# Graph attention in two layers: three row terms as column-tile partial sums, a later end of layer norm, and another order of the first transposes

## The chip, the cores and the metric

The kernel runs on one core of one Trainium2 chip. The metric is the device time of one execution in microseconds; smaller is better. A measured time is the median of several executions of the same program. The profile is of one execution.

## The reference

There are 4096 nodes with 512 features (`x`), an adjacency of zeros and ones (`adj`, 4096 x 4096), and two layers, each followed by adding its input and a layer norm over the 512 features without learned factors.

Layer 0 has 8 heads of 64 features:

```python
feats = jnp.einsum('nf,hfo->hno', X, W)
s_self = jnp.einsum('hno,ho->hn', feats, a_self)
s_neigh = jnp.einsum('hno,ho->hn', feats, a_neigh)
dense = s_self[:, :, None] + s_neigh[:, None, :]
dense = jnp.where(dense > 0, dense, ALPHA * dense)
dense = dense * A[None, :, :]
attn = jax.nn.softmax(dense, axis=-1)
out = jnp.einsum('hij,hjo->hio', attn, feats) + b[:, None, :]
```

Then `x = layernorm(x + relu(out))`. Layer 1 is an attention inside groups of 128 nodes: query, key and value are linear maps of x with biases, and

```python
a = jnp.where(mask, query @ key.T * scale, 0.0)
scores = (a + b + edge_encoding) * jnp.where(mask, 1.0, -1000000.0)
softmax = jax.nn.softmax(scores, axis=-1) * mask
return softmax @ value
```

with `b` and `edge_encoding` both the adjacency. Its result is added to x and normalized again.

## The kernel before, in words

The work lies in `adjacency_streamed_path`; a general path follows only for inputs of another kind and isn't run here. TensorE's instructions stand in the order in which the program was written (`manual_schedule` for that engine). The order on the other engines (VectorE, ScalarE, GpSimd, and SyncE, which issues most loads) is chosen when the program is built, from a model of times[...]. So a change in the text can move instructions on those engines that it doesn't name.

**Setup** (about 0 to 165 us) goes over eight blocks `k` of 512 rows of x. `load_rows` brings four tiles of 128 rows. `turn_rows` (L634) transposes them, chunk of features by chunk (outer loop `c`, inner loop over the four tiles `u`, L637 to L639), and ScalarE copies each chunk to `xT`, adding the row sums into `xs` (L640). `features` (L716, products L719) multiplies `xT` with W and VectorE adds the bias into `fb` (L727). `scores` (L644, products L648) multiplies with `wa`, which VectorE makes at the start from W and the two attention vectors (L628, L631); it puts four products of 32 columns each into four groups of 32 partitions, and ScalarE copies the result to `st` (L656). `exponentials` (L658) sums the four groups with a small product (L662) and takes exponentials. `scaled_features` (L730) makes `gst` and `fst` (ScalarE L741, then VectorE L742), which GpSimd's queue writes to memory (L754). After the last block, sixteen products of one column each (L789) multiply W with the sum `xsum` of all rows of x, four chunks of features for each of four pairs of heads; the result becomes `S_col` (L796). Then the first adjacency tiles are transposed (L1109) and cast by ScalarE to `at` (L1113).

**Four passes** over the adjacency follow (`main_pass`, L1287), one for each pair of heads, each over four chunks of 1024 columns and, inside, over 32 row tiles `j` in cycles of 8 tiles (passes 0 to 2) or 4 (pass 3, then called a group). In each cycle VectorE makes `q` (L1348) for each `j` and each of two heads; ScalarE (and, for one `j` in four and the second head, VectorE) makes a mark from it (L1357, L1353). TensorE computes `accf` from `at` (L1368), `acc` from `q` (L1388), and every eight tiles `dens` from the marks (L1402). There are six buffers for `q` in pass 3 and eight in the others. Between these products other pieces are put in: in pass 1 the weights of layer 1, in passes 1 to 3 the check of the adjacency (loads of `ck`, squares and absolute values on ScalarE, L1128 and L1129).

**Weights of layer 1** (`weights_of_layer_1`, L868) is a generator; `run_pieces` (L1273) takes its next piece while a credit lasts, and the numbers that it yields are what a piece costs of that credit. Its end has three row terms. `zb` is Wk times bq, made with sixteen one-column products (L912). `cb` is bk times bq (L928). `ub` is a row, Wq times bk: four products of 32 columns each put partial sums into four groups of 32 partitions (L932), ScalarE scales and copies them (L936), and one product with a matrix `pick`, which has ones in the rows 0, 32, 64 and 96, adds them into every partition (L943). These three stand in one piece on TensorE, at 951 to 961 us.

**Layer 1** is worked off block by block of 512 rows (`layer_1`, L948) from the second chunk of pass 3 on: as soon as a chunk of 1024 columns is done, its rows are assembled (`rows_of_layer_0`, L1133) in two blocks. There, VectorE takes the statistics and GpSimd the power (L524 to L528); what remains is a function `finish` (L530), which normalizes the four tiles `x1b` in place on VectorE (L532). It is kept as `plan["F"]` (L1145) and called at a place of its own. `layer_1` then transposes `x1b` (L954), ScalarE copies to `x1T` (L955), and products with M (L974), scores (L1001), values (L1046, bias added on VectorE L1054 as `v_t`) and the output (L1060) follow.

Where these pieces go in pass 3 is written out by hand. `PLAN` (L1256) has, for each of the eight groups of a chunk, two strings: what is put in ahead of `acc` and what behind it. `E` ends a chunk, and assembles the first block; `R` assembles the second; `F` calls the kept end of layer norm; `a` and `b` take the next part of the first and second block's layer 1. After the last chunk the same letters stand in one string (L1456).

Of the kernel before, what the change touches and what calls it, by code (L numbers as in the profile page):

```python
# [10 lines left out]
F32 = mybir.dt.float32  # L11
# [3 lines left out]
OP = mybir.AluOpType  # L15
# [4 lines left out]
P = 128  # L20
# [384 lines left out]
def adjacency_streamed_path(  # L405
# [80 lines left out]
    nc.gpsimd.memset(neg_half_4, -0.5)  # L486
    neg_quarter = const.tile([P, 1], F32, name="neg_quarter")
    nc.gpsimd.memset(neg_quarter, -0.25)
    ones_col = const.tile([P, 1], F32, name="ones_col")
    nc.gpsimd.memset(ones_col, 1.0)  # L490
    ident_b = const.tile([P, P], BF16, name="ident_b")
# [60 lines left out]
    def misc(shape, dtype=F32):  # L552

        banks.append(banks.pop(0))
        return banks[-1].tile(shape, dtype, name="ps_m")
# [4 lines left out]
    def ring(name, pool, n):  # L560
# [4 lines left out]
        turns[name] += 1  # L565
        return pool if k < n else more[name][0]

    ats = {}
    a_bs = {}
    pools = {}  # L570
# [11 lines left out]
    with tc.tile_pool(name="setup1", bufs=1, side="right") as one, tc.tile_pool(  # L582
# [50 lines left out]

        def turn_rows(k):  # L634
            xT = xTs[k] = two.tile([P, FC, 4, P], F32, name="xT_f")
            for c in range(FC):
                pt = pss.tile([P, 4, P], F32, name="ps_set")  # L637
                for u in range(4):
                    nc.tensor.transpose(pt[:, u, :], xts[k][u][:, ts(c, P)], ident)  # L639
                nc.scalar.activation(  # L640
                    xT[:, c], pt, AF.Identity, accum_out=xs[:, c, k : k + 1]
                )
# [114 lines left out]
        for k in range(NB):  # L757
            if k + 1 < NB:
                load_rows(k + 1)
            fbs = [features(k, 0)]  # L760
            if k == 0:
                fbs.append(features(k, 1))
                scores(0)
            else:
                exponentials(k)
            if k + 1 < NB:
                turn_rows(k + 1)
            if k == 0:
                exponentials(0)
            scaled_features(k, 0, fbs[0])  # L770
            if k:
                fbs.append(features(k, 1))
                columns_of_exponentials(k - 1)
            scaled_features(k, 1, fbs[1])
            fbs.append(features(k, 2))
            scaled_features(k, 2, fbs[2])
            if k + 1 < NB:
                scores(k + 1)
            rows_of_exponentials(k)
            fbs.append(features(k, 3))  # L780
            scaled_features(k, 3, fbs[3])
            if k in (3, 4, 5):
                tc.keep_in_program_order(load_adjacency(0, 4 * (k - 3)))
        xsum = one.tile([P, FC], F32, name="xsum")
        nc.vector.tensor_reduce(xsum, xs, AX.X, OP.add)
        pS = pss.tile([P, PR], F32, name="ps_set")
        for r in range(PR):
            for c in range(FC):
                nc.tensor.matmul(  # L789
                    pS[:, r : r + 1],  # L790
                    w_sb[:, c, ts(r, FP)],
                    xsum[:, c : c + 1],
                    start=(c == 0),
                    stop=(c == FC - 1),
                )
        nc.vector.scalar_tensor_tensor(  # L796
            S_col, b_col, float(N), pS, op0=OP.mult, op1=OP.add
        )
# [69 lines left out]
    def weights_of_layer_1(keep, wp):  # L868
# [33 lines left out]
        for o in range(FC):  # L902
# [3 lines left out]
            nc.scalar.copy(L1["wvT"][:, :, ts(o, P)], pv)  # L906
            if o % 2:
                yield 1.3
        pz = misc([P, FC])
        for m in range(FC):  # L910
            for o in range(FC):
                nc.tensor.matmul(  # L912
                    pz[:, m : m + 1],
                    ws["k"][:, o, ts(m, P)],
                    cols["q"][:, o : o + 1],
                    start=(o == 0),
                    stop=(o == FC - 1),
                )
        nc.scalar.mul(L1["zb"], pz, scale)
        yield 2.0  # L920

        pc = misc([P, 1])
        kb = wp.tile([P, FC, P], F32, name="kb")
        nc.vector.tensor_copy(kb, cols["k"][:, :, None].to_broadcast([P, FC, P]))

        pu = misc([P, F])
        for o in range(FC):
            nc.tensor.matmul(  # L928
                pc, kb[:, o, :], cols["q"][:, o : o + 1], start=(o == 0), stop=(o == FC - 1)
            )  # L930
        for o in range(FC):
            nc.tensor.matmul(  # L932
                pu[32 * o : 32 * o + 32, :], kb[:, o, :32], ws["q"][:, o, :], start=True, stop=True
            )
        part = ws["v"][:, 0, :]
        nc.scalar.mul(part, pu, scale)  # L936
        pick = ws["v"][:, 1, :P]
        nc.vector.memset(pick, 0.0)
        for o in range(FC):
            nc.vector.memset(pick[32 * o : 32 * o + 1, :], 1.0)  # L940
        yield 2.0
        pu = misc([P, F])
        nc.tensor.matmul(pu, pick, part, start=True, stop=True)  # L943
        nc.scalar.copy(L1["ub"], pu)
        nc.scalar.mul(L1["cb"], pc, scale)
        yield 4.5

    def layer_1(blk, x1b, lp, lp1, lp2):  # L948

# [303 lines left out]

    PLAN = [("E", "Fb"), ("b", "b"), ("b", "a"), ("Ra", "Fa"), ("a", "b"), ("ba", "b")]  # L1256
    PLANS = PLAN + [("ab", ""), ("aaba", "")], PLAN + [("a", ""), ("aa", "a")]
    plan = {"b": None}

# [190 lines left out]
    with tc.tile_pool(name="lp", bufs=2) as lp, tc.tile_pool(  # L1450
        name="lp1", bufs=1
    ) as lp1, tc.tile_pool(name="lp2", bufs=2) as lp2:
        pools.update(lp=lp, lp1=lp1, lp2=lp2)
        main_pass(3)
        plan["K"] = kind_of_inputs(lp1)
        run_plan("bbEFbbbbaaRFaaKKbbababaababbbb")  # L1456


@with_exitstack
# [50 lines left out]
```

## Time and profile before

| what | value |
|---|---|
| median of 3 runs | 2091.82 us (2089.79 to 2091.85) |
| the profiled execution | 2089.37 us, of which its span is 2087.0 us |
| TensorE products | 2055.3 us busy, 15014 records |
| VectorE | 1659.8 us busy |
| ScalarE | 1537.4 us busy |
| GpSimd | 251.0 us busy |
| DMA | 551.28 MB, mean 264 GB/s |
| acc (L1388) | 908.3 us busy, 8192 records |
| accf (L1368) | 494.2 us busy, 2048 records |

The profiler's page and the answers taken from its trace are read like this. A group's row has the line of the kernel, the engine (PE is TensorE's product, PEld its load of weights, DVE VectorE, ACT ScalarE, POOL GpSimd, SP SyncE), the operation, what it writes and reads, how often, busy time, mean time of one, and the idle time ahead of it with what ended that. A row of a list in order of time has the start and the length in us, then the same names; `[2.46 <-DVE q L1348]` at its end means that the engine was idle for 2.46 us ahead of it until q of line 1348 was there. A row of waits has the engine and line that waited, for whom, the sum in us, how often and the longest. A row of a stretch of time has its limits and length, the busy time of PE, PEld, DVE, ACT and POOL with their instructions, then the clock that TensorE was granted as a share of full speed, the DMA engines' share, and GB/s. A product of 32-bit floats makes two records. Products are pipelined, and their ends are modelled: starts are more exact than lengths.

### The profile page before, as it was taken

The page shows a single profiled execution, that of the slowest core. Times are in us where ns is not written, and L with a number is a line of the kernel's source. Part 1 is how long each engine was busy: PE and PEld are TensorE (multiplying, and loading weights), DVE is VectorE, ACT ScalarE, POOL GpSimd, SP SyncE. Part 2 cuts the span into 40 slices and gives each one's busy share as a digit, 9 for nine tenths or more (in the row PEclk, how much of TensorE's full clock was granted, in tenths as well). Part 3 has the DMA queues.
Part 4 walks back from the last instruction along what each step waited for, and adds up shares of the span by engine and source line. Part 5 has one row for each costly group of instructions (what it writes and reads, how often), then busy time and mean ns, then how long its engine had stood idle before and what let it go on. Part 6 is the DMA issues. An engine that isn't in the chain of part 4 may idle for free. (4 is left out here: it accounts for less than half of the span.)

```text
span 2087.0 us, 38127 instructions
## 1 busy us (share of the span) xinstructions
PE 2055.3 (98%) x15014; PEld 1011.8 (48%) x15014; DVE 1659.8 (80%) x2037; ACT 1537.4 (74%) x1819; POOL 251.0 (12%) x393
## 2 busy tenths in 40 slices
PE   8999999999999999999999999999999999999997
PEld 4556555555545444444445444544454444445443
DVE  5556887888798998797999999998975884886654
ACT  3328898888878899787899899998775666567420
POOL 2343222222100000000000000000300210210111
PEclk9999999999999999999999999999999999999999
DMA  8999999999899999897999899989964773775211
GB/s 253 266 258 242 272 292 257 301 255 298 267 334 331 363 335 342 257 312 254 334 310 339 304 350 329 324 290 360 305 238 145 240 255 126 227 272 165 73 48 43
DMA packets 207881, 551.28 MB, mean 264 GB/s; under 512 B 25292, under 2 KB 66252, under 8 KB 207692
## 3 DMA queue, kind: packets, MB, share of 16 engines
q1 hardware_dynamic: 140748, 425.79, 59.0%
q0 software_dynamic: 62784, 121.91, 23.3%
q8 instruction: 120, 1.97, 0.4%
q10 hardware_dynamic: 4160, 1.05, 0.2%
q14 instruction: 69, 0.57, 0.1%
HBM read 491.79 MB, written 107.22 MB: 287 GB/s over the span
## 5 line engine op out<-in xcount | busy, mean ns | idle before, releaser
L1348 DVE SCALAR_TENSOR_TENSOR q<-p_row,d_all,at 128x1024 f32<-128x1024 f32 x1024 | 1242.5, 1278 | 170.2 <-PE acc L1388 142.0
L1357 ACT ACTIVATE mark<-q,nb_all 128x1024 fp8e4<-128x1024 f32 x896 | 995.8, 1145 | 191.4 <-DVE q L1348 175.3
L1388 PE MATMUL acc<-q,g_s 128*32 128x512 f32 x8192 | 908.3, 594 | 3.2 <-DVE q L1348 2.9
L1388 PEld LDWEIGHTS acc<-q,g_s 128*32 128x32 f32 x8192 | 265.4, 110 | 601.3 <-issue 534.2
L1368 PE MATMUL accf<-at,f_s 128*128 128x512 f32 x2048 | 494.2, 397 | 1.9 <-issue 1.8
L1368 PEld LDWEIGHTS accf<-at,f_s 128*128 128x128 f32 x2048 | 379.8, 189 | 111.0 <-issue 29.1
L1128 ACT ACTIVATE ck<-ck,neg_half_f 128x1024 f32<-128x1024 f32 x128 | 146.0, 1141 | 21.1 <-DMA ck<-in_adj_dram 21.0
L1129 ACT ACTIVATE ck<-ck,neg_quarter 128x1024 f32<-128x1024 f32 x128 | 146.4, 1143 | 1.8
L1113 ACT CAST at<-ps_m 128x1024 fp32r<-128x1024 fp8e4 x128 | 120.2, 1026 | 10.9 <-issue 5.9
L1402 PE MATMUL dens<-mark,e_b 128*6 128x512 fp8e4 x2048 | 124.6, 379 | 0.0
L719 PE MATMUL ps_set<-w_sb_f,xT_f 128*128 128x512 f32 x256 | 116.0, 601 | 0.0
L974 PE MATMUL ps_m<-x1T,M_sb 128*128 128x512 f32 x256 | 113.1, 595 | 1.2 <-ACT x1T L955 1.2
L1046 PE MATMUL ps_m<-wvT,x1T 128*128 128x512 f32 x256 | 114.2, 594 | 0.0
L1233 POOL DMA_DIRECT2D hs_d<-hst x12 | 10.7, 894 | 841.9 <-DVE hst L1223 641.3
L1353 DVE TENSOR_SCALAR mark<-q,d_all 128x1024 fp8e4<-128x1024 f32 x128 | 95.8, 749 | 4.8
L1402 PEld LDWEIGHTS <-e_b 128*6 128x6 bf16 x2048 | 52.5, 86 | 79.4 <-issue 35.3
L1114 POOL DMA_DIRECT2D at_d<-at x128 | 68.7, 537 | 167.8 <-ACT at L1113 108.1
L741 ACT ACTIVATE fst<-fb 128x512 fp32r<-128x512 f32 x32 | 20.4, 637 | 86.1 <-DVE fb L727 52.1
L974 PEld LDWEIGHTS ps_m<-x1T,M_sb 128*128 128x128 f32 x256 | 47.9, 190 | 62.7 <-issue 59.9
L1046 PEld LDWEIGHTS ps_m<-wvT,x1T 128*128 128x128 f32 x256 | 47.6, 190 | 57.2 <-issue 56.0
L719 PEld LDWEIGHTS ps_set<-w_sb_f,xT_f 128*128 128x128 f32 x256 | 48.9, 198 | 49.5 <-issue 49.1
L1054 DVE TENSOR_TENSOR v_t<-ps_m,bv_row 128x512 f32<-128x512 f32 x32 | 21.9, 684 | 62.2 <-PE ps_m L1046 62.2
(177 smaller groups left out, 1136.6 us busy)
## 6 DMA issues: line engine op xcount, KB each, us to landing
at<-at_d SPq DMA_DIRECT2D x384, 512.0 KB, 6.0
ck<-in_adj_dram SPq DMA_DIRECT2D x128, 512.0 KB, 5.4
f_s<-f_d SPq DMA_DIRECT2D x128, 512.0 KB, 7.5
at_d<-at POOLq DMA_DIRECT2D x128, 512.0 KB, 14.7
g_s<-g_d SPq DMA_DIRECT2D x128, 256.0 KB, 5.7
f_d<-fst POOLq DMA_DIRECT2D x32, 512.0 KB, 7.7
p_row<-pu_d SPq DMA_DIRECT2D x32, 512.0 KB, 6.8
a_b<-in_adj_dram POOLq DMA_DIRECT2D x32, 512.0 KB, 16.3
```

The source lines that it names most:

```text
L719: nc.tensor.matmul(pf, tile_j(xTs[k][:, c].rearrange("p u n -> p (u n)"), u), w_sb[:, c, :], start=(c == 0), stop=(c == FC - 1),)
L974: nc.tensor.matmul(pz, L1["M"][:, f, ts(c, P)], x1T[:, f, :], start=(f == 0), stop=(f == FC - 1),)
L1046: nc.tensor.matmul(pv, x1T[:, f, ts(u, P)], L1["wvT"][:, f, :], start=(f == 0), stop=(f == FC - 1),)
L1113: nc.scalar.copy(at, both[:, :, k])
L1128: tc.keep_in_program_order(nc.scalar.activation(ck, ck, AF.Square, bias=neg_half))
L1129: nc.scalar.activation(ck, ck, AF.Abs, bias=neg_quarter, accum_out=binp[:, k : k + 1])
L1348: nc.vector.scalar_tensor_tensor(q, p_row[h], d_j, ats[r, c, j].bitcast(F32), op0=OP.max, op1=OP.mult)
L1353: nc.vector.tensor_scalar(mark, q, d_j, None, op0=OP.is_gt, saturate=False)
L1357: nc.scalar.activation(mark, q, AF.Sigmoid, bias=nb_all[:, j, hh : hh + 1], scale=BIG, saturate=False,)
L1368: nc.tensor.matmul(accf[:, s, :], f_s[j // 4][:, j % 4, w, :], ats[r, c, j][:, ts(s, HB)], start=(j == 0 and w == 0), stop=(j == NT - 1 an ...
L1388: nc.tensor.matmul(acc[o : o + 32, s, :], g_s[j // 4][:, j % 4, h, o % FH : o % FH + 32], qs[j, h][:, ts(s, HB)], start=(j == 0), stop=(j ...
L1402: nc.tensor.matmul(dens[lo : lo + 6, :], e_b[:, j, 2 * r + h, :], marks[j, h][:, ts(s, HB)], start=(j == 0), stop=(j == NT - 1),)
```

## The change

It has four parts.

1. `partial_sums` and `sums_to_columns` are new. The row sum of setup (`S_col`) is made with four products of 32 columns ahead of the last block's last features, a copy by ScalarE, and four one-column products that add the partial sums; the sixteen one-column products go. For that there is a new constant `pick_col`.
2. `zb` and `ub` of layer 1 are made the same way, with two sets of four products in one piece; the sum of the partial rows and columns comes in a later piece. `cb` stays. The sixteen one-column products for `zb` go, and the cost that is yielded changes.
3. In the first block the transposes go tile by tile instead of chunk by chunk; the later blocks keep their order.
4. The letter F goes two places later in `PLAN`, for the first block from behind acc of the group 0 to behind acc of the group 1, for the second from behind acc of the group 3 to ahead of acc of the group 4; and it goes later in the last string.

```diff
+    pick_col = const.tile([P, 1], F32, name="pick_col")
+    nc.vector.memset(pick_col, 0.0)
+    for c in range(FC):
+        nc.vector.memset(pick_col[32 * c : 32 * c + 1, :], 1.0)
...
+    def partial_sums(dst, wide, rhs):
+        for c in range(FC):
+            nc.tensor.matmul(
+                dst[32 * c : 32 * c + 32, :], wide[:, c, :32], rhs[:, c, :], start=True, stop=True
+            )
+
+    def sums_to_columns(dst, part):
+        for m in range(FC):
+            nc.tensor.matmul(
+                dst[:, m : m + 1], part[:, ts(m, P)], pick_col, start=True, stop=True
+            )
...
         def turn_rows(k):
             xT = xTs[k] = two.tile([P, FC, 4, P], F32, name="xT_f")
+            pts = {}
+            order = [(u, c) for u in range(4) for c in range(FC)]
+            for u, c in order if k == 0 else sorted(order, key=lambda x: x[1]):
+                if u == 0:
+                    pts[c] = pss.tile([P, 4, P], F32, name="ps_set")
+                nc.tensor.transpose(pts[c][:, u, :], xts[k][u][:, ts(c, P)], ident)
             for c in range(FC):
-                pt = pss.tile([P, 4, P], F32, name="ps_set")
-                for u in range(4):
-                    nc.tensor.transpose(pt[:, u, :], xts[k][u][:, ts(c, P)], ident)
+                pt = pts[c]
...
             rows_of_exponentials(k)
+            if k == NB - 1:
+                xsum = one.tile([P, FC], F32, name="xsum")
+                nc.vector.tensor_reduce(xsum, xs, AX.X, OP.add)
+                xsum_b = one.tile([P, FC, 32], F32, name="xsum_b")
+                nc.vector.tensor_copy(xsum_b, xsum[:, :, None].to_broadcast([P, FC, 32]))
+                pS = pss.tile([P, H * FH], F32, name="ps_set")
+                partial_sums(pS, xsum_b, w_sb)
+                S_part = one.tile([P, H * FH], F32, name="st")
+                nc.scalar.copy(S_part, pS)
             fbs.append(features(k, 3))
...
-        xsum = one.tile([P, FC], F32, name="xsum")
-        nc.vector.tensor_reduce(xsum, xs, AX.X, OP.add)
         pS = pss.tile([P, PR], F32, name="ps_set")
-        for r in range(PR):
-            for c in range(FC):
-                nc.tensor.matmul(
-                    pS[:, r : r + 1],
-                    w_sb[:, c, ts(r, FP)],
-                    xsum[:, c : c + 1],
-                    start=(c == 0),
-                    stop=(c == FC - 1),
-                )
+        sums_to_columns(pS, S_part)
...
-        pz = misc([P, FC])
-        for m in range(FC):
-            for o in range(FC):
-                nc.tensor.matmul(
-                    pz[:, m : m + 1],
-                    ws["k"][:, o, ts(m, P)],
-                    cols["q"][:, o : o + 1],
-                    start=(o == 0),
-                    stop=(o == FC - 1),
-                )
-        nc.scalar.mul(L1["zb"], pz, scale)
-        yield 2.0
         pc = misc([P, 1])
         kb = wp.tile([P, FC, P], F32, name="kb")
         nc.vector.tensor_copy(kb, cols["k"][:, :, None].to_broadcast([P, FC, P]))
-        pu = misc([P, F])
         for o in range(FC):
             nc.tensor.matmul(
                 pc, kb[:, o, :], cols["q"][:, o : o + 1], start=(o == 0), stop=(o == FC - 1)
             )
-        for o in range(FC):
-            nc.tensor.matmul(
-                pu[32 * o : 32 * o + 32, :], kb[:, o, :32], ws["q"][:, o, :], start=True, stop=True
-            )
-        part = ws["v"][:, 0, :]
-        nc.scalar.mul(part, pu, scale)
-        pick = ws["v"][:, 1, :P]
-        nc.vector.memset(pick, 0.0)
-        for o in range(FC):
-            nc.vector.memset(pick[32 * o : 32 * o + 1, :], 1.0)
+        nc.scalar.mul(L1["cb"], pc, scale)
+        qb = ws["v"][:, 2, :P].rearrange("p (c n) -> p c n", c=FC)
+        nc.vector.tensor_copy(qb, cols["q"][:, :, None].to_broadcast([P, FC, 32]))
+        pick = ws["v"][:, 3, :P]
+        nc.vector.tensor_copy(pick, pick_col.to_broadcast([P, P]))
+        parts = []
+        for i, (wide, rhs) in enumerate(((kb, ws["q"]), (qb, ws["k"]))):
+            pu = misc([P, F])
+            partial_sums(pu, wide, rhs)
+            parts.append(ws["v"][:, i, :])
+            nc.scalar.mul(parts[i], pu, scale)
+        yield 6.0
+        pu = misc([P, F])
+        nc.tensor.matmul(pu, pick, parts[0], start=True, stop=True)
+        nc.scalar.copy(L1["ub"], pu)
+        pz = misc([P, FC])
+        sums_to_columns(pz, parts[1])
+        nc.scalar.copy(L1["zb"], pz)
         yield 2.0
-        pu = misc([P, F])
-        nc.tensor.matmul(pu, pick, part, start=True, stop=True)
-        nc.scalar.copy(L1["ub"], pu)
-        nc.scalar.mul(L1["cb"], pc, scale)
-        yield 4.5
...
-    PLAN = [("E", "Fb"), ("b", "b"), ("b", "a"), ("Ra", "Fa"), ("a", "b"), ("ba", "b")]
+    PLAN = [("E", "b"), ("b", "Fb"), ("b", "a"), ("Ra", "a"), ("Fa", "b"), ("ba", "b")]
...
-        run_plan("bbEFbbbbaaRFaaKKbbababaababbbb")
+        run_plan("bbEbbFbbaaRaFaKKbbababaababbbb")
```

In the changed kernel the four products of `partial_sums` stand in line 576, and those of `sums_to_columns` in line 583.

## The prediction

> **What bounds the kernel now.** I read the page's busy line first, then TensorE's own waits, then the stretches that the change touches: TensorE, VectorE and ScalarE in order of time, with the granted clock.
>
> ```profile
> PE 2055.3 (98%) x15014; PEld 1011.8 (48%) x15014; DVE 1659.8 (80%) x2037; ACT 1537.4 (74%) x1819; POOL 251.0 (12%) x393
> PE ps_set L639 <- DMA xt_f<-in_x_dram: 7.0, 4, 4.2
> PE acc L1388 <- DVE q L1348: 2.9, 3, 2.5
> PE ps_m L1060 <- DVE v_t L1054: 1.8, 1, 1.8
> PE ps_m L943 <- ACT w_v L936: 0.7, 1, 0.7
> ```
>
> TensorE is the bound: 98% busy, its named waits sum to about 19 us. So time is won where TensorE issues less, waits less, or isn't slowed; on another engine only where TensorE waits for it. Four stretches hold the change. The first is the row terms of layer 1, TensorE in order of time and then the clock (the column after five engines' busy time) of three stretches of it:
>
> ```profile
> 951.31 3.63 PE L912 MATMUL ps_m<-b_q,w_k 128*128 128x1 f32 x32
> 954.80 1.20 PE L928 MATMUL ps_m<-b_q,kb 128*128 128x1 f32 x8
> 955.93 1.93 PE L932 MATMUL ps_m<-w_q,kb 128*32 128x512 f32 x8
> 958.58 2.08 PE L943 MATMUL ps_m<-w_v 128*128 128x512 f32 x2 [0.72 <-ACT w_v L936]
> 960.58 14.79 PE L1388 MATMUL acc<-q,g_s 128*32 128x512 f32 x128
> 951.30:954.80 3.50, 3.50 (x34) 3.49 (x32) 0.00 (x0) 0.00 (x0) 0.00 (x0) 1.00 0.99 365
> 956.00:958.00 2.00, 1.86 (x8) 0.12 (x8) 0.00 (x0) 1.28 (x3) 0.00 (x0) 0.50 0.19 76
> 960.60:963.00 2.40, 2.40 (x17) 0.65 (x20) 0.00 (x0) 2.28 (x3) 0.00 (x0) 0.64 0.65 217
> ```
>
> After 3.5 us of one-column products the clock is halved, and L932, L943 and the start of acc pay for it. Next, setup's end: the same kind of product, then transposes, then accf at half clock (9.87 us for 32 records; later cycles take 7.60):
>
> ```profile
> 159.51 3.63 PE L789 MATMUL ps_set<-xsum,w_sb_f 128*128 128x1 f32 x32
> 168.14 1.01 PE L1109 MATMUL ps_m<-ident_b,a_b 128*128 128x128 bf16 x8 [0.82 <-ACT at L1113]
> 168.91 9.87 PE L1368 MATMUL accf<-at,f_s 128*128 128x512 f32 x32
> ```
>
> Third, the first layer-norm end in the last pass: VectorE waits for GpSimd, normalizes, and only then makes the q that TensorE waits for:
>
> ```profile
> 1488.98 1.26 DVE L1348 SCALAR_TENSOR_TENSOR q<-p_row,d_all,at 128x1024 f32<-128x1024 f32 x1
> 1491.49 1.91 DVE L532 TENSOR_SCALAR x1b<-x1b,mv_f,rstd_f 128x512 f32<-128x512 f32 x4 [1.26 <-POOL rstd_f L528]
> 1493.32 8.45 DVE L1348 SCALAR_TENSOR_TENSOR q<-p_row,d_all,at 128x1024 f32<-128x1024 f32 x7
> 1494.66 7.46 PE L1388 MATMUL acc<-q,g_s 128*32 128x512 f32 x46 [2.46 <-DVE q L1348]
> 1508.07 7.07 PE L1388 MATMUL acc<-q,g_s 128*32 128x512 f32 x64
> ```
>
> Last, the start, where the copy st is what the first small product L662 needs:
>
> ```profile
> 21.47 0.63 ACT L741 ACTIVATE fst<-fb 128x512 fp32r<-128x512 f32 x1 [9.30 <-DVE fb L727]
> 22.01 0.57 ACT L656 COPY st<-ps_set 128x512 f32<-128x512 f32 x1
> 23.68 1.01 PE L662 MATMUL ps_set<-stack,st 128*128 128x16 f32 x8
> ```
>
> [...] one-column products that fill the busy column don't keep the clock. [...] L789 and the next line start 3.56 us apart, 32 records, 111 ns each. [...] scores (L648) does 8 records of 32x512 in 1.06 us where L719 takes 3.69 for 8 of 128x512. [...]
>
> **The change part by part.** On TensorE the built order differs only in the products below; everything else keeps its place, so the changed yields (8.5 to 8.0) shift no other piece.
>
> Row terms of layer 1. Before, from the end of accf (951.31) to the next dens (975.20): 23.89 us. After, first call: L928's 8 records stay, 1.13; two partial sums at the rate of scores (28.15 to 29.15, 1.00 each) 2.0; acc at full clock 13.8 (928.27 to dens at 942.03). Second call, one group later: the row product, 2 records, 0.86 (half of L1060's 1.72 for four); four column products, 8 records of 0.111, 0.89. Sum 18.7, gain 5.2. The wait for ACT (0.72) goes because a group lies between. If the column tiles ran one after the other, 16 records of 0.43 (L719's step) would cost 4.9 more; I take side by side. Ends: 3.5 and 5.7. ACT gets one more copy of 0.6 in a stretch where it waited 4.7 us; VectorE's copies replace memsets.
>
> Row sum of setup. Goes: 3.56. Comes: 1.00 + 0.89. Net 1.67 at the transposes. But accf waits for ACT's casts (7.54 us for eight), and ACT's order now has the last fst (0.57 in a row) behind the first cast: the fourth transpose group starts at 162.65 + 0.57 + 4 x 0.94 = 167.0 instead of 168.1. Gain 1.1 if the clock falls for the same length. If the half-rate end keeps its moment, half of that is lost; if the clock never falls, 2.3 more. I take 0.9; ends 0.4 and 3.4.
>
> First end of layer norm, second column chunk. It moves behind seven q. Eight q from 1487.72 at 1.21 end at 1497.5; with the last 16 acc records (1.75) acc ends at 1499.2, before 1502.4: 3.2. What is late next: the four normalizations (1.83) and a mark (0.67) now stand before the next group's q, which end at 1500.0 + 9.7 = 1509.7; that acc could end at 1511.9 by TensorE's own count and needs 1511.5 by the q, against 1515.07. The transposes that read x1b come at about 1512, 12 us after it. Then L974 waits for x1T behind one more mark on ACT: 0.4 to 1.0 back. I take 2.5; ends 0.5 and 3.3.
>
> The same in the third and fourth chunks. There acc took 8.10 instead of 7.07 us (at 1658), its last q at 1664.4. In the new order one normalization pair and no wait for GpSimd stand before that q: 1663.7. Gain 0.6 twice, 1.2; ends 0 and 1.8. The other block's end (1706.41, wait 1.24) costs TensorE nothing now, since acc comes at 1720.4; moved behind six q, it ends at about 1715.5, and the transposes come at 1727.4. Nothing. GpSimd's power and the DMAs aren't moved.
>
> The end after the last chunk: three normalizations instead of four stand before v_t: 0.45 of L1060's 1.84; ends 0 and 0.5.
>
> First rows tile by tile. The last tile lands at 8.41; 4 instead of 13 transposes follow, so features start 1.5 and end about 1.0 us earlier. But scores needs wa, whose last reduction on VectorE ends at 20.84 and is not touched: nothing is won. And ACT's order now has two fst before st: the second needs fb, made on VectorE after the first fst (22.14 + 0.62 + 0.62 = 23.4). So st starts at about 24.0 instead of 22.0, L662 at 24.6 instead of 23.68, and TensorE has no slack after it: a loss of 1.0; ends 0 and 2.7[...]. pick_col's five memsets lie in VectorE's 7.7 us of waiting for a_self.
>
> Sum: 5.2 + 0.9 + 2.5 + 1.2 + 0.45 - 1.0 = 9.25. The profiled execution took 2089.37 (span 2087.0), so 2080.1; the median of the runs is 2.45 above it, and the forecast for a median is 2091.82 - 9.25 = **2082.6**.
>
> **The rivals.** *The stall moves one group on*: the last-pass ends win nothing, because VectorE's load per group is the limit. For: at 1636 acc is late with no normalization in sight. Against: in the same chunk acc takes 7.0 at 1548 and 1564. 9.25 - 3.7 gives 2086.3. *The clock is kept at setup's end*: the one-column stretch is a quarter as long. Against: the transposes between are half idle. 2082.6 - 2.4 = 2080.2. *The partial sums run one after the other*: 4.9 and 2.4 lost, 2089.9; L648 speaks against it. *Slower, through SP's queue*: after the row terms one load of ck comes before an f_s load, and SP waits for ACT to free ck (112.5 us in 44 waits between 940 and 1340, the longest 7.8). Place: the 17 wide cycles from 963 on. Price: what f_s comes late after its slack (issued 987.15, landing 7.5 later, read at about 1004.1: 9.4 us). It decides if TensorE idles 0.8 us in each cycle: 13.6 lost, 2096. Against: the order differs in one cycle only, and there ACT's check comes earlier too.
>
> **How the numbers follow.** Forecast 0.61, stall moves on 0.17, clock kept 0.12, one after the other 0.04, SP's queue 0.06. About 0.2% (4.2 us) is what a measurement can tell from no change, so faster means below 2087.6: 0.61 + 0.12 + 0.13 = 0.86; the rest of the second case and the fourth make the same, 0.08; slower 0.06. The range goes from 2077.5 (clock kept, upper ends) to 2087.5 (stall moves on, lower ends).
>
> **What would show it.** Row terms: no half clock near 955, acc 13.9 us there, one-column products in eights. Setup: the gap from the last features to accf 1.5 to 2 us shorter. Last pass: no wait of acc for q near 1490, no half clock after it; acc next at 7.0. Start: L662 waits about 1 us for st. I am wrong if TensorE's waits grow in the wide passes, if acc in the last pass waits a group later, or if L576 takes more than 1.1 us for 8.

## The result, and the profile after

The changed kernel takes 2080.91 us (median of 6 runs, 2079.42 to 2083.51) against 2091.22 us before (6 runs in the same series, 2089.79 to 2092.61). The ratio is 0.9952, with a 95% interval of 0.9942 to 0.9963: faster by 10.3 us. The forecast of 2082.6 had 9.25 us. That the total fits doesn't mean that each term did: some were too small, and a loss that I had not forecast made up for them.

The profiled execution of the changed kernel is its slowest, 2083.51 us with a span of 2080.8. So the two profiles differ by only 6.2 us. First TensorE's own waits on the changed kernel (line, what it waited for, us in total, times, the longest):

```profile
PE ps_m L1122 <- ACT at L1126: 3.0, 2, 1.8
PE dens L1415 <- ACT mark L1370: 2.7, 5, 0.7
PE ps_m L967 <- DVE tot L884: 2.3, 1, 2.3
PE ps_m L1073 <- DVE v_t L1067: 1.4, 1, 1.4
PE ps_set L686 <- ACT st L680: 0.8, 1, 0.8
PE acc L1401 <- DVE q L1361: 0.4, 2, 0.2
```

The wait of 2.5 us for q is gone. New are the waits of dens for marks, a longer one of L967 for tot in the tail, and the forecast one for st. The wait for the casts at setup's end (L1122) grew from 1.4 to 3.0 us, since the transposes now come earlier.

**Row terms of layer 1.** The timeline of the changed kernel, TensorE alone (start, duration, line, operation):

```profile
955.76 0.95 PE L937 MATMUL ps_m<-b_q,kb 128*128 128x1 f32 x8
956.64 1.07 PE L576 MATMUL ps_m<-w_q,kb 128*32 128x512 f32 x8
957.52 1.04 PE L576 MATMUL ps_m<-w_k,w_v 128*32 128x512 f32 x8
958.38 13.92 PE L1401 MATMUL acc<-q,g_s 128*32 128x512 f32 x128
...
981.39 1.02 PE L954 MATMUL ps_m<-w_v 128*128 128x512 f32 x2
982.26 0.95 PE L583 MATMUL ps_m<-pick_col,w_v 128*128 128x1 f32 x8
```

The windows view of two stretches of it, from L937 on and from the start of acc (the clock is the column after the five engines):

```profile
955.80:957.60 1.80, 1.80 (x21) 1.19 (x23) 0.00 (x0) 0.17 (x1) 0.00 (x0) 1.00 0.77 284
958.40:961.00 2.60, 2.60 (x32) 0.81 (x28) 0.63 (x1) 2.34 (x3) 0.00 (x0) 1.00 0.81 309
```

Eight records in four column tiles step on by 0.88 and 0.86 us, the clock stays at 1.00, and acc takes 13.92 instead of 14.79 us.

**Setup's end.** TensorE alone, and the windows view of the stretch in which its clock was halved:

```profile
157.13 1.07 PE L576 MATMUL ps_set<-w_sb_f,xsum_b 128*32 128x512 f32 x8
158.12 3.71 PE L743 MATMUL ps_set<-w_sb_f,xT_f 128*128 128x512 f32 x8
161.67 0.95 PE L583 MATMUL ps_set<-pick_col,st 128*128 128x1 f32 x8
...
166.05 0.61 PE L1122 MATMUL ps_m<-ident_b,a_b 128*128 128x128 bf16 x8 [1.82 <-ACT at L1126]
167.87 1.01 PE L1122 MATMUL ps_m<-ident_b,a_b 128*128 128x128 bf16 x8 [1.22 <-ACT at L1126]
168.64 9.85 PE L1381 MATMUL accf<-at,f_s 128*128 128x512 f32 x32
...
166.80:173.50 6.70, 5.63 (x20) 4.56 (x20) 6.70 (x7) 6.67 (x8) 2.94 (x7) 0.50 0.98 360
```

The partial sums stand ahead of the last features, and only eight one-column records are left behind them. The later transposes wait for ScalarE's casts, and accf still falls into the half clock.

**First end of layer norm.** VectorE's timeline on the changed kernel:

```profile
1486.46 8.43 DVE L1361 SCALAR_TENSOR_TENSOR q<-p_row,d_all,at 128x1024 f32<-128x1024 f32 x7
1494.81 0.54 DVE L537 TENSOR_SCALAR x1b<-x1b,mv_f,rstd_f 128x512 f32<-128x512 f32 x1
```

And TensorE's, with the windows view of a part of it:

```profile
1486.98 9.44 PE L1401 MATMUL acc<-q,g_s 128*32 128x512 f32 x62
...
1502.36 7.07 PE L1401 MATMUL acc<-q,g_s 128*32 128x512 f32 x64
1509.36 1.09 PE L967 MATMUL ps_m<-ident_f,x1b 128*128 128x128 f32 x8
...
1522.86 7.11 PE L987 MATMUL ps_m<-x1T,M_sb 128*128 128x512 f32 x16 [0.85 <-ACT x1T L968]
...
1489.00:1498.00 9.00, 8.57 (x82) 2.35 (x80) 9.00 (x11) 8.63 (x17) 1.79 (x2) 1.00 0.97 331
```

Normalizing (L537) stands behind the q. acc still takes 9.4 us for 62 records, since it follows VectorE's q one by one, but it has no hole and no half clock. The next acc takes 7.07: the stall has not moved on.

In the third chunk acc took 8.10 us in the kernel before and takes 7.07 in the changed one:

```profile
1658.23 8.10 PE L1388 MATMUL acc<-q,g_s 128*32 128x512 f32 x64
...
1652.69 7.07 PE L1401 MATMUL acc<-q,g_s 128*32 128x512 f32 x64
```

**Start.** ScalarE's timeline on the changed kernel has a second fst ahead of st:

```profile
23.38 0.63 ACT L765 ACTIVATE fst<-fb 128x512 fp32r<-128x512 f32 x1 [1.36 <-DVE fb L751]
23.92 0.57 ACT L680 COPY st<-ps_set 128x512 f32<-128x512 f32 x1
```

TensorE waits for wa, and then for st:

```profile
20.82 1.05 PE L672 MATMUL ps_set<-xT_f,wa 128*32 128x512 f32 x2 [1.34 <-DVE wa L650]
24.54 1.12 PE L686 MATMUL ps_set<-stack,st 128*128 128x16 f32 x8 [0.78 <-ACT st L680]
```

**Stages of all profiled executions.** Since totals of single executions vary by 2 us and more, I cut each profiled execution at products that every version has. Start: when L686 of block 0 starts. Setup: from there to the first acc. Layer 0: from there to the accf that starts at 692.01 in the kernel before. Rows: from the accf at 943.87 to the second dens after it (998.51). Pass: from there to the last dens (1964.40). Tail: from there to the start of the last group of products. The 251.9 us between layer 0 and rows are the same within 0.1 in all. "Half" is how long the records of the granted clock show 0.5 at setup's end. All in us.

| kernel | start | setup | half | layer 0 | rows | pass | tail |
|---|---|---|---|---|---|---|---|
| before | 23.68 | 155.94 | 10.24 | 512.39 | 54.64 | 965.89 | 108.80 |
| b_wide_pz | 23.63 | 156.51 | 10.24 | 513.07 | 51.89 | 965.65 | 109.29 |
| b_rows | 23.53 | 154.79 | 6.83 | 513.38 | 48.80 | 965.33 | 109.96 |
| changed | 24.54 | 154.79 | 6.83 | 517.12 | 48.76 | 959.85 | 110.02 |
| a_again | 25.10 | 155.10 | 6.83 | 514.80 | 48.80 | 959.37 | 109.38 |
| a_chunks | 23.82 | 154.28 | 6.83 | 514.44 | 48.78 | 960.08 | 108.88 |
| a_oldplan | 24.67 | 155.94 | 6.83 | 512.51 | 48.76 | 964.94 | 110.28 |
| a_second_old | 24.84 | 153.67 | 3.41 | 512.72 | 48.76 | 960.07 | 109.36 |
| a_setup_old | 24.40 | 156.49 | 10.24 | 514.98 | 48.80 | 960.20 | 109.41 |
| a_wa_early | 23.69 | 154.25 | 6.83 | 514.05 | 48.80 | 959.98 | 108.95 |
| a_fill | 24.84 | 154.00 | none | 513.79 | 48.76 | 960.10 | 109.68 |
| a_klate | 25.21 | 153.73 | 3.41 | 514.59 | 48.78 | 960.92 | 107.78 |
| a_best | 24.14 | 152.07 | none | 516.07 | 48.80 | 960.92 | 107.78 |
| a_best2 | 23.39 | 152.71 | none | 511.86 | 48.79 | 959.34 | 107.76 |

The names are those of the experiments below. Between the first row and "changed": 0.9 lost at the start, 1.15 won in setup, 4.7 lost in layer 0, 5.9 won in the row terms, 6.0 in the pass, 1.2 lost in the tail; 6.2 in all. Of the 6.0 of the pass, 1.1 lie ahead of the first end that was moved: from the accf at 1375.97 to the one at 1473.00 the kernel before took 97.0 us and the changed one 95.9, and the fourteen executions take 95.5 to 97.0 us there, with no order by version.

### The profile page after: what moved, and what is told of

It is laid out like the page before. It is cut to its first block, busy times and chain, and to the rows that moved or that the text cites. A ratio compares the mean times of both kernels' runs of the same rounds, so it can differ in the third digit from the quotient of the medians.

```text
span 2080.8 us, 38068 instructions
## 1 busy us (share of the span) xinstructions
PE 2045.7 (98%) x14982; PEld 1005.3 (48%) x14982; DVE 1660.4 (80%) x2040; ACT 1536.7 (74%) x1821; POOL 246.4 (12%) x393
## 4 chain that ended last, share of the span: by engine, by line
PE 83%; DMA 7%; issue 4%; DVE 2%; ACT 2%; POOL 1%; SPq 0%; POOLq 0%; ACTq 0%; DVEq 0%
PE acc L1401 36%; PE accf L1381 20%; PE ps_set L743 5%; PE ps_m L1059 5%; DMA at_d<-at 5%; PE ps_m L987 5%; PE dens L1415 5%; PE ps_m L1014 1%; PE ps_m L1073 1%; ACT mark L1370 1%; DVE q L1361 1%; PE ps_m L1122 1%; PE ps_m L916 1%; DMA f_s<-f_d 1%; DMA hs_d<-hst 1%
## 5 line engine op out<-in xcount | busy, mean ns | idle before, releaser
L743 PE MATMUL ps_set<-w_sb_f,xT_f 128*128 128x512 f32 x256 | 116.9, 605 | 0.1
L987 PE MATMUL ps_m<-x1T,M_sb 128*128 128x512 f32 x256 | 113.1, 595 | 1.6 <-ACT x1T L968 1.6
L987 PEld LDWEIGHTS ps_m<-x1T,M_sb 128*128 128x128 f32 x256 | 47.9, 190 | 63.1 <-issue 60.1
L743 PEld LDWEIGHTS ps_set<-w_sb_f,xT_f 128*128 128x128 f32 x256 | 49.0, 199 | 51.3 <-issue 49.9
L994 ACT ACTIVATE zT<-ps_m,zb 128x512 f32<-128x512 f32 x32 | 21.8, 683 | 70.3 <-PE ps_m L987 70.3
```

Source lines behind the costliest of these rows:

```text
L743: nc.tensor.matmul(pf, tile_j(xTs[k][:, c].rearrange("p u n -> p (u n)"), u), w_sb[:, c, :], start=(c == 0), stop=(c == FC - 1),)
L987: nc.tensor.matmul(pz, L1["M"][:, f, ts(c, P)], x1T[:, f, :], start=(f == 0), stop=(f == FC - 1),)
```

## The experiments

Ratios are to the kernel before, run on the same chip, with 95% intervals. "a" versions start from the changed kernel, "b" versions from the one before. By their totals only a_oldplan and a_best2 lie clear of the changed kernel among the "a" versions; what the others show is read from their traces, one execution each.

### Row terms: all of them alone, and the clock alone

b_rows is the kernel before with the changed `weights_of_layer_1`, `pick_col` and the two helpers, and nothing else.

> The kernel before with the new row terms of layer 1 alone (pick_col and the two helpers included, one-column row sum of setup, old places of the ends, old order of the first rows). My prediction gave them 5.2 us, the traces of the two kernels 5.9: 2085.3 to 2086. From dens to dens the stretch goes from 23.9 to about 18 us, with no half clock at 955 but still one at setup's end and one near 1495. Rival (part of the 5.9 came from a phase of the clock that the earlier changes set): 4 us or less.

Measured: 2087.06 us, ratio 0.9978 (0.9970 to 0.9986), about 1 us above what was expected. The stage takes 48.80 instead of 54.64 us: 5.84, as in every execution with the new row terms. The rival falls.

b_wide_pz keeps the old way and only makes the one-column products 128 columns wide:

```diff
-        pz = misc([P, FC])
+        qw = ws["v"][:, 2, :].rearrange("p (c n) -> p c n", c=FC)
+        nc.vector.tensor_copy(qw, cols["q"][:, :, None].to_broadcast([P, FC, P]))
+        pz = misc([P, FC, P])
...
-                    pz[:, m : m + 1],
+                    pz[:, m, :],
                     ws["k"][:, o, ts(m, P)],
-                    cols["q"][:, o : o + 1],
+                    qw[:, o, :],
```

> The kernel before, with the 32 one-column products of the row term zb made 128 columns wide (the same column of q repeated)[...]; one VectorE copy is added and only the first of the 128 columns is used. Theory A (the clock falls because the array hardly streams in the one-column products, though TensorE's busy column is full): the stretch takes 3.5 to 5 us, no half clock follows it, the two partial-sum products and acc take 1.1 + 0.9 + 13.9 us instead of 1.9 + 1.4 + 14.8, so 2 us are won there if the stretch stays at 3.6 us (2089), less what it grows by. Theory B (the clock falls for another cause at that place, a wait or a load): half clock again at about 956, and the time is 2091 or more.

Measured: 2089.26 us, ratio 0.9983 (0.9975 to 0.9992). TensorE's timeline there:

```profile
952.50 3.73 PE L914 MATMUL ps_m<-w_v,w_k 128*128 128x128 f32 x32
956.07 0.95 PE L930 MATMUL ps_m<-b_q,kb 128*128 128x1 f32 x8
...
959.86 13.94 PE L1390 MATMUL acc<-q,g_s 128*32 128x512 f32 x128
```

The windows view of a part of it:

```profile
955.00:957.00 2.00, 2.00 (x24) 1.99 (x25) 0.00 (x0) 0.17 (x1) 0.00 (x0) 1.00 0.98 387
```

128 times the columns take about as long (3.73 us for 32 records, with one column 3.63), and the clock stays at 1.00. The stage gets shorter by 2.75 us (54.64 to 51.89). So what theory A expected came, and theory B falls; what the array does inside such a product isn't in the traces. Of the 5.84 us of the row terms, 2.75 are the clock that the one-column products let fall, and 3.1 are products and a wait that went. The split rests on the traces, for the intervals of the two totals overlap.

### The ends of layer norm: both back, then the second alone

a_oldplan has both places and the last string as before, a_second_old only the second block's place:

```diff
# a_oldplan
-    PLAN = [("E", "b"), ("b", "Fb"), ("b", "a"), ("Ra", "a"), ("Fa", "b"), ("ba", "b")]
+    PLAN = [("E", "Fb"), ("b", "b"), ("b", "a"), ("Ra", "Fa"), ("a", "b"), ("ba", "b")]
# a_second_old
+    PLAN = [("E", "b"), ("b", "Fb"), ("b", "a"), ("Ra", "Fa"), ("a", "b"), ("ba", "b")]
```

> The changed kernel with both layer-norm ends back in their old places, as in the kernel before. My theory: the 2.5 us wait of acc for q comes back at the first end, with 3.3 us lost in the second chunk, 0.9 in each of the third and fourth, and 0.4 at v_t in the tail; of the tail's 0.4 nothing reaches the end, because the transposes L967 wait for tot. Sum 5.1 slower without the tail, 2086. In the tail L967's wait for tot goes from 2.3 to about 0.5 us, which gives up to 1.5 back: 2084.5. Rival (the gain of the last pass came from the earlier row terms and not from the places): no wait of acc for q above 0.5 us, 2081.

Measured: 2086.21 us, ratio 0.9977 (0.9969 to 0.9986). The hole is back in TensorE's timeline, and from its end on the half clock, 3.41 us long (the last line is from the windows view):

```profile
1489.02 7.46 PE L1401 MATMUL acc<-q,g_s 128*32 128x512 f32 x46 [2.46 <-DVE q L1361]
...
1488.90:1492.20 3.30, 3.18 (x14) 1.11 (x18) 3.30 (x4) 3.30 (x11) 2.77 (x1) 0.50 0.88 288
```

Against the changed kernel 3.2 us are lost in the second chunk (0.15 of them come back at L987), 1.0 each in the third and fourth, and 0.45 at v_t. The last part of the expectation failed: L967's wait for tot stayed at 2.1 us instead of 0.5. It is 0.4 to 2.1 us long in the four executions with the old ends and 1.1 to 2.3 in seven with the new ones and the count in its old place, so no effect of the ends' place on it can be told.

> The changed kernel with only the second layer-norm end of each chunk in its old place (the first end stays two places later). My prediction gave the second end nothing, since acc came 14 us after it. So: no change, 2081, and TensorE's products in the last pass at the same distances within 0.2 us. Rival (the second end carries part of the 0.9 us that the third and fourth chunks won each): up to 1.8 us slower, 2082.7.

Measured: 2078.92 us, ratio 0.9937 (0.9922 to 0.9952), and the pass takes 960.07 us, among 959.4 to 960.2 of most others. So the second end carries nothing. The total is 2 us below the changed kernel's, which the intervals don't separate; the profiled execution is shorter than the changed kernel's by 1.1 us in setup and 4.4 in layer 0, which the edit doesn't touch.

### The start: old order of the transposes, and an earlier wa

a_chunks has the transposes of the first block chunk by chunk again:

```diff
-            for u, c in order if k == 0 else sorted(order, key=lambda x: x[1]):
+            for u, c in sorted(order, key=lambda x: x[1]):
```

> The changed kernel with its first rows turned chunk by chunk again; nothing else differs. My theory: the tile-by-tile order lets the first features start 1.8 us earlier, but scores still waits for wa, and ScalarE's order gets a second fst ahead of st. So with chunks L686 starts at about 23.7 instead of 24.54 and the kernel is 0.9 us faster (about 2080.0 against 2080.9). Rival (the early start is worth something later, since the first features and their stores come sooner): L686 at 23.7, but what follows doesn't keep the gain, or the time gets longer by up to 1 us. By the trace the difference is to be seen at L686 and unchanged at the last features of setup.

Measured: 2080.85 us, ratio 0.9955 (0.9938 to 0.9972). L686 has no wait for st:

```profile
23.82 1.01 PE L686 MATMUL ps_set<-stack,st 128*128 128x16 f32 x8
```

It starts at 23.82 instead of 24.54 us (25.10 when the changed kernel was profiled once more), and the last features of setup still start 0.82 us earlier (157.30 instead of 158.12). So the trace shows the loss of the tile-by-tile order, 0.7 to 1.3 us; the total is too coarse for it.

a_wa_early issues two loads on another queue:

```diff
         for k, v in enumerate((a_self, a_neigh)):
-            nc.sync.dma_start(
+            nc.gpsimd.dma_start(
```

> The changed kernel with the loads of a_self and a_neigh issued on GpSimd's queue instead of SP's, where they stand behind four tiles of x. My theory: wa is what scores waits for (1.3 us), so with the two loads landing 2 to 4 us earlier wa is ready when the first features end: L672 doesn't wait, L686 comes 1.3 us earlier or more, at 23.2 or sooner, and the tile-by-tile order of the first rows pays at last; 1 to 2 us faster than the changed kernel. Rival A (the weights w_sb land last, or GpSimd's queue brings the loads as late): L672 still waits above 1 us. Rival B (wa is early, but st stands behind the second fst): L672 doesn't wait and L686 does, for st, by as much.

Measured: 2079.80 us, ratio 0.9953 (0.9936 to 0.9969). L672 no longer waits for wa and L686 not for st, but the last tile of x now comes late (its transposes wait 2.15 us for it), and the features start at 12.51 instead of 9.47 us; L686 at 23.69. None of the theories foresaw that: of what the loads of `a_self` and `a_neigh` won, the loads of x lost a part. Of the 1.3 us expected, 0.9 are left.

### Setup's end: the old row sum, and the clock kept by fillers

a_setup_old has the one-column row sum again:

```diff
-                partial_sums(pS, xsum_b, w_sb)
...
-        sums_to_columns(pS, S_part)
+        for r in range(PR):
+            for c in range(FC):
+                nc.tensor.matmul(
+                    pS[:, r : r + 1],
+                    w_sb[:, c, ts(r, FP)],
+                    xsum[:, c : c + 1],
+                    start=(c == 0),
+                    stop=(c == FC - 1),
+                )
```

> The changed kernel with setup's row sum as before (32 one-column products, no partial sums). My theory: TensorE comes to the transposes 1.5 us later (0.95 + 1.07 against 3.56), ScalarE's last fst goes ahead of the casts again, and the first acc comes 0.9 to 1.2 us later if the half clock lasts as long, 6.8 us. [...] where it lasts 10.2 us, as in the kernel before, accf stays at half clock to its end in either case. By the time: 0.9 to 2.5 slower than the changed kernel. Rival (the casts set the first accf alone, so that the products ahead of the transposes are hidden): first acc at the same place, no difference.

Measured: 2082.65 us, ratio 0.9955 (0.9939 to 0.9972); setup takes 156.49 us, against 153.7 to 155.9 us, 154.5 on average, in seven executions with the new row sum and no fillers. Counted from L686, the first transposes come 1.9 us later than in the changed kernel's first profile (140.25 and 138.36 us) and accf 1.6 us (145.72 and 144.10). So the products ahead of the transposes are not hidden by the casts. The total doesn't show it: its interval holds the changed kernel's ratio.

a_fill adds products between the first transposes, while TensorE waits for casts:

```diff
                         bring(0, 0, j)
+                        for i in range({2: 12, 4: 8}.get(j, 0)):
+                            nc.tensor.matmul(
+                                acc[:, 0, ts(i % 4, P)], ident, ident, start=True, stop=True
+                            )
```

> The changed kernel with 20 more products of 128 columns between the first transposes of the first pass, while TensorE waits there for ScalarE's casts (12 after the second transpose group, 8 after the third), written to a buffer that the real products overwrite from their start. Theory A (the half clock at setup's end comes from the idle stretch, 3 us of waits among 5 us of transposes): the clock stays full, accf takes 7.6 instead of 9.85 us, 2.2 us faster, 2078.7. Theory B ([...] the fillers are too few, or they start too late): the clock falls at another moment, between no gain and 2 us. Theory C (the fillers delay the transposes and so the casts): accf later by up to 1 us.

Measured: 2078.69 us, ratio 0.9941 (0.9925 to 0.9958). The fillers and accf in TensorE's timeline:

```profile
164.98 2.90 PE L1351 MATMUL acc<-ident_f 128*128 128x128 f32 x24
...
170.42 7.58 PE L1385 MATMUL accf<-at,f_s 128*128 128x512 f32 x32
```

accf takes 7.58 instead of 9.85 us, and the half clock at setup's end is gone. But a filler is two records, 0.24 us, so they were longer than the waits, and accf starts 7.83 us behind L583 instead of 6.97: 0.86 later. So theory A held for the clock, and theory C for the number of fillers.

### The tail, and the parts together

a_klate makes the flag's count, KK, three letters later:

```diff
-        run_plan("bbEbbFbbaaRaFaKKbbababaababbbb")
+        run_plan("bbEbbFbbaaRaFabbaKKbabaababbbb")
```

> The changed kernel with the count of the flag (its product with okp and the three small VectorE steps on tot) one transpose group and two steps later in the tail. My theory: in the tail L967 doesn't wait for its own rows but for the buffer of that product, which is free only when VectorE, behind a normalization and four products with ub, has added it to tot; so the wait of 1.1 to 2.3 us that L967 shows for tot goes to 0.4 or less, and the time falls by 1 to 2 us (2079 to 2080). Rival (the rows themselves are late, since their load arrives about 28 us after hst): L967 waits as long for x1b or x1T, and the time stays at 2081.

Measured: 2078.99 us, ratio 0.9937 (0.9923 to 0.9950). L967 in the timeline of the changed kernel:

```profile
2010.96 1.53 PE L967 MATMUL ps_m<-ident_f,x1b 128*128 128x128 f32 x12 [2.27 <-DVE tot L884]
```

And on a_klate:

```profile
2006.06 2.07 PE L967 MATMUL ps_m<-ident_f,x1b 128*128 128x128 f32 x16
```

The wait is gone and the tail takes 107.8 us in all three versions with the later count, against 108.9 to 110.0 in seven without: 1.6 us on average. So L967 was held up by the count: both take their buffers from the same pool (`misc`), and the next transposes could start only when VectorE had added the count to tot.

a_best joins a_chunks, a_klate and 11 fillers (7 and 4). a_best2 adds a buffer of its own for ScalarE's copy of ae, and a_again is the changed kernel once more, beside it.

```diff
-            aes = hp_.tile([P, CT, FP], F32, name="hst")
-            aes = aes.rearrange("p t n -> p (t n)")[:, :HB]
+            aes = pools["aes"].tile([P, HB], F32, name="aes")
```

> The changed kernel with three edits: first rows chunk by chunk again, the flag's count later in the tail, and 11 products of 128 columns between the first transposes (7 and 4; each took 0.24 us), overwritten from the start of acc. If the parts add up: 0.8 from the start, 1 to 2 from the tail, and 2.2 from the full clock with no delay of accf (20 of them delayed accf by 0.85 us and still won 1.4 by the trace), 4 to 5 in all: 2076 to 2077. Rival for the fillers (11 are too few): the clock is halved again for 3.4 or 6.8 us after 166, accf 8.6 to 9.9 us, 2078 to 2079.

Measured: 2078.43 us, ratio 0.9932 (0.9918 to 0.9946). Setup takes 152.07 us: 11 fillers are enough for the clock and delay nothing (accf starts 6.63 us behind L583). The total missed 2076 to 2077; the profiled execution spent 516.07 us in layer 0, 1.6 more than the average of the "a" versions. There ScalarE's copy waits for an earlier store from the same buffer, as its timeline on the changed kernel shows:

```profile
393.00 0.58 ACT L1185 COPY hst<-ae 128x512 f32<-128x512 f32 x1 [5.47 <-DMA hs_d<-hst]
```

On a_best2, with a buffer of its own, it doesn't:

```profile
377.68 0.59 ACT L1184 COPY aes<-ae 128x512 f32<-128x512 f32 x1
```

> The changed kernel itself, once more, beside the last version. Its profiled execution lost 4.4 us between 390 and 700 us, where ScalarE's copy of ae waited 5.5, 4.9 and 3.0 us for the store of hst and the marks came late; other executions of the same stretch of code waited 3.1 to 4.7. Theory (that wait differs from execution to execution): the local times of everything that the change touches come again within 0.3 us, the loss in that stretch differs, and the span differs by it, by the half clock at setup's end[...] and by L967's wait for tot. Median 2079 to 2082.

> The changed kernel with first rows chunk by chunk, the flag's count later in the tail, 11 products between the first transposes, and a buffer of its own for the copy of ae, which so far shares the one buffer of hst and waits for its store. By the traces: 0.8 from the start, 2.1 from the tail, 2.3 from the full clock, and 1 to 4 from the marks that are no longer late in layer 0: 6 to 9 in all against the changed kernel in the same runs, 2072 to 2075. Rival (the store of hst only moves its wait, now to VectorE's write of the next hst): 2076 to 2077, with VectorE waiting for the store instead.

Measured, in one series: a_again 2080.80 us, ratio 0.9945 (0.9931 to 0.9958); a_best2 2075.75 us, ratio 0.9915 (0.9900 to 0.9931). In a_again the rows and the pass come again within 0.5 us, but start and tail differ by 0.6, twice what was expected, and layer 0 by 2.3. In a_best2 the copy no longer waits for the store, VectorE doesn't wait for it in its place, and layer 0 takes 511.86 us, the shortest of all. a_best2 is 5 us faster than the changed kernel by the medians, and 8.7 by the stages of the two traces (its profiled execution is its fastest); the median missed 2072 to 2075 by a little.

## Why the prediction was right, by its steps

- **Row terms, 5.2 forecast, 5.84 measured.** The step held: the clock stays at 1.00, and eight records of L576 step on by 0.88 us, where eight of L743 take 3.55 (158.12 to 161.67 us). The prices of the products were too high: L937 steps on by 0.88 us, not 1.13, and the two partial sums by 1.74, not 2.0; acc took 13.7 of the 13.8 forecast.
- **Setup's row sum, 0.9 forecast, about 1.4 measured** (155.9 us on average in four executions with the old one: before, b_wide_pz, b_rows, a_setup_old; 154.5 in the seven with the new one and no fillers). The first transposes come 1.7 us earlier on average, counted from L686, as forecast; the casts took back 0.3 of that, not 0.57. The step on the clock had too simple a picture. The records show 10.24 us of half clock in three of the four and 6.83 or 3.41 in the seven, but the shorter stretch begins later: 1.89 us ahead of accf in the changed kernel (166.75 us) and 5.29 in the kernel before (163.62). From the start of accf to the first acc it is 10.71 us in the kernel before and 10.77 in a_setup_old, and 10.69 in the changed one, 10.63 in a_again and 10.25 in a_wa_early: 0.2 less on the average of these, and the last three alone differ by 0.4. So a gain from the clock can't be told. One execution can be off by 1 us here.
- **First end, 2.5 forecast, 3.0 measured** (3.2 in the second chunk, 0.15 lost again behind it). The forecast times of acc were exact: L967 behind the next acc starts at 1509.36, which is 1511.9 on the old time scale (2.54 us had been won up to there), as forecast. What was too large is the price for L974 (now L987): it waits 0.4 us longer, but only 0.15 of it reached what follows.
- **Third and fourth chunks, 1.2 forecast, 2.0 measured** (1.02 and 0.99 in a_oldplan). Both acc there take 7.07 us now. In the third chunk the last q ends at 1657.74, which is 1663.3 on the old time scale: 1.1 us earlier, not the 0.7 of the forecast. The second end is worth nothing, as forecast.
- **Tail, 0.45 forecast, 0.2 measured, less than the executions differ by.** v_t's wait fell from 1.84 to 1.38 us as forecast. But the step failed to ask what is late next: L967's wait for tot, 0.4 to 2.3 us long, takes up what is won ahead of it. Old ends: 109.6 us on average (before, b_wide_pz, b_rows, a_oldplan), new ends with the count in its place 109.4. In the one profile that I had, that wait was only 0.44 us:

```profile
2017.70 1.09 PE L954 MATMUL ps_m<-ident_f,x1b 128*128 128x128 f32 x8 [0.44 <-DVE tot L861]
```

- **First rows, loss of 1.0 forecast, 1.1 measured** (L686 at 24.80 us on average in seven executions with the tiles' order and the loads as they were, 23.70 in six with the chunks' order), for the reason given: st at 23.92 (forecast 24.0), L686 at 24.54 (forecast 24.6).
- **Not forecast: layer 0.** It takes 512.4 to 513.4 us in the three executions of the kernel before and its "b" versions, and 511.9 to 517.1 in the eleven others, 514.5 on average without a_best2. TensorE waits there for marks behind ScalarE's copy of ae, which waits up to 5.5 us for a store. The stretch from the accf at 381.75 to the one at 407.55 follows that wait: 25.8 us where the copy waited 3.1, 26.1 at 3.5, 27.4 at 4.8 and 28.1 at 5.5. Shown is also that a buffer of its own removes the wait. Open is whether the change makes the store later: five executions have the changed kernel's code up to there (changed, a_again, a_oldplan, a_second_old, a_klate) and took 512.5 to 517.1.

The sum of the stages' averages, executions with the old way of a stage against those with the new: 1.1 lost at the start, 1.4 won in setup, 5.9 in the row terms, 5.4 in the pass, 0.2 in the tail, 1.6 lost in layer 0. That is 10.2, against 10.3 by the medians. My terms were short by 2.5 us, and layer 0 gave most of that back: that the total came as close as it did is in part luck.

Of the rivals, three are refuted by the traces: acc after the first end takes 7.07 us (no stall moved on), eight partial-sum records step on by 0.88 us (not one after the other), and the clock did fall at setup's end (0.50 for 6.83 us). The sign for setup was met only in part: the last features and accf stand 2.3 us closer, not 1.5 to 2, because the partial sums went ahead of those features. Against a slower SP queue speaks that the distance between the two kernels' products stays at 1.42 us from 984 to 1415 us.

## What to carry to other kernels

A sum over an axis that lies on partitions was cheaper here as wide products in column tiles with one small product behind them than as a row of one-column products, and about half of the gain (2.75 of 5.84 us in the row terms) came from the clock that the latter let fall for the work behind them. When a step is moved, ask for each engine what stands next to it in the order, and for each win what the next wait absorbs; a wait that looks small in one profile can be several times as long in the next (L967's for tot: 0.4 to 2.3 us). To judge parts of a microsecond, cut the traces at products that all versions share, and use the medians only for the sum.

## What the runs showed of the hardware

- A full busy time of TensorE doesn't mean a full clock: in the kernel before, 32 records of 128x1 fill 3.5 us and the clock falls to 0.50 behind them; in b_wide_pz, 32 of 128x128 take about the same time (3.73 us) and it stays at 1.00.
- A hole of 2.46 us in TensorE's work was followed by half clock twice: in the kernel before, where TensorE was busy for 0.94 us between 1491.4 and 1494.8 us and the clock was 0.50 from 1494.82 us on for 3.41, and in a_oldplan, where acc stopped at 1486.56 us, went on at 1489.02, and the clock was 0.50 from about 1488.9 us on. Without the hole, in the changed kernel, the clock is 1.00 there. At the changed kernel's setup end TensorE was busy for 1.38 us between 163.35 and 166.75 us, and the half clock begins at 166.75.
- At setup's end the half clock lasted 6.83 or 10.24 us with the old row sum, and 3.41 or 6.83 with the new. What sets its start and its length is not shown. From the start of accf to the first acc it is 10.25 to 10.77 us in the five executions named above for setup's row sum, and 8.42 without a half clock (a_fill and a_best2).
- 11 fp32 products of 128 columns (22 records), put into waits, kept the clock in both executions that had them (a_best and a_best2: no half clock at setup's end); in a_best2, accf took 7.58 us instead of 9.85.
- A store moves TensorE through ScalarE: where the copy of ae waited 5.47 instead of 3.45 us for it, in two executions of the changed kernel, TensorE's stretch there took 28.1 instead of 26.1 us.
